# A selective scan that reads delta·u·B from PSUM, with B broadcast as three bfloat16 parts

## The chip, the cores and the metric

The kernel runs on one core of one Trainium2 chip. The metric is the device time of one execution in microseconds (us). Unless said otherwise, a time is the median of the runs of one kernel, and all runs used here are of the fast state. TensorE is called PE, its weight loads PEld, VectorE DVE, ScalarE ACT, GpSimd POOL. The granted clock is the share of TensorE's full clock that the profile records as granted; every entry of the record in the two traces before and after is 1 or 0.5, and a mean over a stretch lies between.

## The reference, cut to what matters

The block normalizes, projects and convolves its input, runs a selective scan in four directions (K = 4) over 4096 positions, and ends in linear attention and a quantized FFN. The argument touches only the scan:

```python
def step(h, inps):                       # for each position, N = 16 states n
    d_t, u_t, b_t, c_t = inps            # delta, u, B, C
    h = h * jnp.exp(d_t[..., None] * A) + (d_t * u_t)[..., None] * b_t[:, :, None, :]
    y = jnp.einsum('bkdn,bkn->bkd', h, c_t)
    return (h, y)
```

## The kernel before

Three passes: pass 1 makes u, B, C and the inputs of delta; pass 2 scans; pass 3 is the rest. Pass 2 works in 96 *steps*. A step is 128 (batch, channel) rows, one direction and T = 2048 positions. Each step has 16 *states* n, and halfway through it prepares the next step (delta, delta·u). A pair of batches gives three chunks of 128 rows; "third chunk" below is the one that holds rows of both batches.

```python
for n in range(N):
    if n == N // 2 and at + 1 < len(steps):
        ...
        ready = prepare(next_u, *steps[at + 1])       # delta, delta * u of the next step
    ct = more.tile([P, T], F32, name="ct")            # C's row n, broadcast by DMA
    ...
    da = two.tile([P, T], F32, name="da")
    nc.scalar.activation(da, delta, AF.Exp, scale=a_neg[:, ty, k, n : n + 1])
    dbu = two.tile([P, T], F32, name="dbu")                            # SBUF
    for hf in range(2):
        pb = ps.tile([P, HT], F32, name="pb", tag="wide")              # PSUM: B on all partitions
        for q in range(0, HT, GRP):
            nc.tensor.matmul(pb[:, q : q + GRP], spread(n, c), xd[...], start=True, stop=True)
        nc.vector.tensor_mul(dbu[:, sub], du[:, sub], pb)
    h = two.tile([P, T], F32, name="h")
    nc.vector.tensor_tensor_scan(h[:, way], da[:, way], dbu[:, way], init, ALU.mult, ALU.add)
    ...
    nc.gpsimd.tensor_mul(ct, ct, h)
    late.append(partial(sum_over_n, acc, ct, n, ...))  # PE adds ct into acc, LAG = 2 states late
```

`sum_over_n` is four fp32 matmuls of 512 columns by an identity matrix, which the profile counts as eight instructions (12,288 for the 1,536 states). "The sums" below are these.

Of the kernel before, what the change touches and what calls it, by code (L numbers as in the profile page):

```python
"""VSS block (group norm, gated depthwise conv, four-direction selective scan) followed by a linear
attention block and an e5m2/fp16-quantized FFN, on one core.

Three passes with DRAM scratch between them, in float32 throughout (e5m2 operands and float16
results where the reference quantizes to those formats):
  1. per pair of batches, channels on partitions: group norm, in_proj, conv + silu -> u; x_proj -> dt,
     B, C in each direction's scan order; silu(z) with tokens on partitions.
  2. per chunk of 128 (batch, channel) rows: the four scans, one state n at a time along the free
     axis. ScalarE makes exp(delta*A), TensorE broadcasts B over partitions and sums h*C over n in
     PSUM, VectorE scans, GpSimd multiplies by C. Reversed directions scan through reversed views.  # L10
  3. per batch, tokens on partitions: layer norm, gate, out_proj, residual; attention without
     softmax, reassociated: y = [ln,1] (Wq blockdiag(Wk^T [ln,1]^T[ln,1] Wv) Wff) + bff; quantized FFN.

A pair's 2*192 channel rows are three chunks of 128: (b0, 0:128), (b1, 0:128), and channels 128:192 of
both (b0 in the lower half). "Type" 0 / 1 below are parameters of channels 0:128 / 128:192 twice.
"""
# [9 lines left out]
F32 = mybir.dt.float32  # L26
F16 = mybir.dt.float16
F8 = mybir.dt.float8e5
AF = mybir.ActivationFunctionType
ALU = mybir.AluOpType  # L30
PSUM = bass.MemoryType.PSUM
DRAM = bass.MemoryType.DRAM

P = 128
NB, HH, WW, C = 8, 64, 64, 96
L = HH * WW
DI, N, R, K = 192, 16, 6, 4
NXD = R + 2 * N
NBLK = L // P
T = 2048  # L40
# [10 lines left out]
def chunk_rows(pair, c):  # L51
    """(partition slice, batch, channel slice) of a chunk's parts."""
    b0 = 2 * pair
    if c < 2:
        return [(slice(0, P), b0 + c, slice(0, P))]
    return [(slice(64 * j, 64 * j + 64), b0 + j, slice(P, DI)) for j in range(2)]


def load_by_type(nc, dst, src):
    """dst [128, 2, ...] from src [192, ...]: channels 0:128, and 128:192 twice."""  # L60
    nc.sync.dma_start(dst[:, 0], src[0:P])
    nc.sync.dma_start(dst[0:64, 1], src[P:DI])
    nc.sync.dma_start(dst[64:P, 1], src[P:DI])


@with_exitstack
def vss_attn_ffn_kernel(ctx: ExitStack, tc: tile.TileContext, g: dict, out: bass.AP):
    nc = tc.nc
    consts = ctx.enter_context(tc.tile_pool(name="consts", bufs=1))
    dram = ctx.enter_context(tc.tile_pool(name="scratch", bufs=1, space=DRAM))  # L70

    ident = consts.tile([P, P], F32, name="ident")
    make_identity(nc, ident)
    mhalf = consts.tile([P, NBLK], F32, name="mhalf")
    nc.vector.memset(mhalf, -0.5)

    u_d = [dram.tile([DI, L], F32, name=f"u_d{b}") for b in range(NB)]
    y_d = [dram.tile([DI, L], F32, name=f"y_d{b}") for b in range(NB)]
    z_d = [dram.tile([P, NBLK, DI], F32, name=f"z_d{b}") for b in range(NB)]
    xd_d = [[dram.tile([2 * NXD, L], F32, name=f"xd_d{b}_{o}") for o in range(2)] for b in range(NB)]  # L80

    def rsqrt_eps(var, eps):
        """var <- (var + eps) ** -0.5"""
        nc.gpsimd.tensor_scalar(var, var, eps, None, ALU.add)  # L84
        nc.gpsimd.tensor_tensor(var, var, mhalf[0 : var.shape[0], 0 : var.shape[1]], ALU.pow)  # L85

    pass1(tc, g, consts, ident, rsqrt_eps, u_d, z_d, xd_d)
    pass2(tc, g, ident, u_d, xd_d, y_d)
    pass3(tc, g, ident, rsqrt_eps, y_d, z_d, out)


@with_exitstack
def pass1(ctx, tc, g, consts, ident, rsqrt_eps, u_d, z_d, xd_d):
    nc = tc.nc
    wp = ctx.enter_context(tc.tile_pool(name="p1w", bufs=1))
    big = ctx.enter_context(tc.tile_pool(name="p1big", bufs=1))
    two = ctx.enter_context(tc.tile_pool(name="p1two", bufs=2))
    ps = ctx.enter_context(tc.tile_pool(name="p1ps", bufs=2, space=PSUM))

# [18 lines left out]
    for pair in range(NB // 2):  # L118
# [64 lines left out]
        for j in range(2):  # L183
            b = 2 * pair + j
            half = slice(64 * j, 64 * j + 64)
            for o in range(2):
# [13 lines left out]
                nc.sync.dma_start(xd_d[b][o], xd)  # L200


@with_exitstack
def pass2(ctx, tc, g, ident, u_d, xd_d, y_d):
    nc = tc.nc
    ND = R + N
    HT = T // 2
# [16 lines left out]
    load_by_type(nc, dt_b, g["dt_biasT"])  # L224
    # Rows as in the xd tile below: (dt, B) of batch 0, then of batch 1.
    dt_w = wp.tile([2 * ND, 3, K, P], F32, name="dt_w")
    nc.vector.memset(dt_w, 0.0)
    src = g["dt_wT"]
    nc.sync.dma_start(dt_w[0:R, 0], src[:, :, 0:P])
    nc.sync.dma_start(dt_w[ND : ND + R, 1], src[:, :, 0:P])  # L230
    nc.sync.dma_start(dt_w[0:R, 2, :, 0:64], src[:, :, P:DI])
    nc.sync.dma_start(dt_w[ND : ND + R, 2, :, 64:P], src[:, :, P:DI])

    spread2 = wp.tile([2 * ND, N, P], F32, name="spread2")
    for j in range(2):
        rows = ident[0 : 2 * ND, j * ND + R : (j + 1) * ND]
        nc.vector.tensor_copy(spread2[:, :, 64 * j : 64 * j + 64], rows.unsqueeze(2).to_broadcast([2 * ND, N, 64]))

    def spread(n, c):
        """Stationary operand that puts B's row n of a chunk's batches on all of their partitions."""  # L240
        if c < 2:
            row = c * ND + R + n
            return ident[0 : 2 * ND, row : row + 1].to_broadcast([2 * ND, P])
        return spread2[:, n, :]

    def piece(t, o, pc):
        """A piece of a [P, L] tile in row-major order, in the direction's order."""
        if o == 0:
# [10 lines left out]
    def prepare(u, pair, c, k, pc):  # L259
        """What a piece's states share: (dt, B) rows of its batches, delta, delta * u."""  # L260
        o, row0, cols = k % 2, (k // 2) * NXD, slice(pc * T, (pc + 1) * T)
        xd = two.tile([2 * ND, T], F32, name="xd")
        for j in range(2):
            nc.sync.dma_start(xd[j * ND : (j + 1) * ND, :], xd_d[2 * pair + j][o][row0 : row0 + ND, cols])
        # delta = softplus(v) = max(v, 0) + log1p(exp(-|v|)), the latter as
        # ln(w) + (e - (w - 1)) with w = 1 + e rounded.
        bias = dt_b[:, c // 2, k : k + 1]
# [17 lines left out]
        nc.gpsimd.tensor_mul(du.rearrange("p (a b) -> p a b", b=HH), delta.rearrange("p (a b) -> p a b", b=HH), piece(u, o, pc))  # L285
        return xd, delta, du

# [8 lines left out]
    ]  # L296
    # The sums over n are issued late, so that TensorE's broadcasts for the next states do not
    # stand behind them.
    late = []
    next_u = load_u(0, 0)  # L300
    ready = prepare(next_u, *steps[0])
    for at, (pair, c, k, pc) in enumerate(steps):
# [7 lines left out]
        if first:  # L310
            carry = two.tile([P, N], F32, name="carry")
        xd, delta, du = ready
        acc = ps_acc.tile([P, T], F32, name="acc")
        for n in range(N):
# [4 lines left out]
            ct = more.tile([P, T], F32, name="ct")  # L319
            row = (k // 2) * NXD + ND + n  # L320
            for part, b, _ in parts:
# [3 lines left out]
            nc.scalar.activation(da, delta, AF.Exp, scale=a_neg[:, ty, k, n : n + 1])  # L325
            dbu = two.tile([P, T], F32, name="dbu")
            for hf in range(2):
                pb = ps.tile([P, HT], F32, name="pb", tag="wide")
                for q in range(0, HT, GRP):
                    nc.tensor.matmul(pb[:, q : q + GRP], spread(n, c), xd[:, hf * HT + q : hf * HT + q + GRP], start=True, stop=True)  # L330
                sub = slice(hf * HT, (hf + 1) * HT)
                nc.vector.tensor_mul(dbu[:, sub], du[:, sub], pb)  # L332
            h = two.tile([P, T], F32, name="h")
            way = slice(None, None, -1) if rev else slice(None)
            init = 0.0 if first else carry[:, n : n + 1]
            nc.vector.tensor_tensor_scan(h[:, way], da[:, way], dbu[:, way], init, ALU.mult, ALU.add)  # L336
            if not final:
# [14 lines left out]
def pass3(ctx, tc, g, ident, rsqrt_eps, y_d, z_d, out):  # L352
# [43 lines left out]
    def normalize(dst, src, st, width, eps):  # L396
        """dst <- layer norm of src [P, blocks, width], from its bn_stats st [P, blocks, 6]."""
        nb = src.shape[1]
# [12 lines left out]
    for b in range(NB):  # L411
# [49 lines left out]

        # Attention without softmax.
        ln = two.tile([P, NBLK, CA], F32, name="ln")
# [37 lines left out]

        # FFN: e5m2 operands, float16 results.
        lf = two.tile([P, NBLK, CA], F32, name="lf", tag="ln")
# [71 lines left out]
```

## Time and profile before

| | us |
|---|---|
| whole kernel, median of 2 runs | 19,455.6 (19,454.37 to 19,456.82) |
| up to the first scan | 1,376 |
| pass 2, from the start of the first scan to the end of the last | 16,314 |
| one step of 16 states | 170 |
| a scan of 2048: alone / beside POOL | 4.48 / 6.57 |

Almost everything is pass 2. The busy times of that stretch, from the table of windows (columns: stretch, its length, busy time and number of instructions of PE, PEld, DVE, ACT and POOL, granted clock, DMA share, GB/s):

```profile
1376.00:17690.00 16314.00, 13637.42 (x25319) 5161.20 (x25318) 13842.94 (x4891) 4458.98 (x3453) 9915.15 (x2215) 0.82 0.34 104
```

PE and DVE are both busy about 84% of it, and neither figure can be taken at its word. A scan that stands still for POOL counts as busy (the prediction shows it): 6.57 us beside a POOL product, 4.48 alone. This standing still is called *the lock* below, a name for what was measured and for no mechanism. And PE's busy time depends on the clock it was granted: the matmul instructions of the sums start 0.429 us apart at full clock and 0.853 at half (medians, from 2,000 to 14,000 us).

### The profile page before, as it was taken

Reading aid. Unit: us, or ns where it says so; the run is one execution under the profiler, and the core shown is the slowest. Engines: PE = TensorE matmul, PEld = TensorE weight load, DVE = VectorE, ACT = ScalarE, POOL = GpSimd, SP = SyncE. Lnnn points to the kernel's source line nnn. Section 1 sums busy time; section 2 is a strip of 40 time slices with the busy share of each in tenths; the row PEclk is TensorE's granted clock in tenths of the full one; section 3 lists DMA queues with packets and bytes.
Section 4 is the critical chain, followed back from the end, with each engine's and each line's share of the span. In section 5 each row is a group of like instructions: output and inputs, shape, how many; then the busy total and the mean of one; then the engine's idle time right before and its main releaser. Section 6 shows DMA issues by size and latency. Waiting matters only on the chain. (4 is left out here: it accounts for less than half of the span.)

```text
span 19457.8 us, 87704 instructions
## 1 busy us (share of the span) xinstructions
PE 15569.7 (80%) x31520; PEld 6174.6 (32%) x31520; DVE 15130.4 (78%) x8039; ACT 5060.0 (26%) x4444; POOL 10511.8 (54%) x2562
## 2 busy tenths in 40 slices
PE   6668888888888888888888888888888888886555
PEld 2123333333333333333333333333333333333443
DVE  4448888888888888888888888888888888885344
ACT  2222222222222222222222222222222222221111
POOL 0016666655666665566666566666655666663323
PEclk5558888888888888888888888888888888886555
DMA  2112232244432322344322222444223223443110
GB/s 73 60 71 106 100 108 102 103 106 101 109 102 102 106 101 104 108 104 101 106 102 103 108 99 109 102 102 106 101 104 108 103 100 103 100 101 89 46 41 26
DMA packets 303310, 1860.89 MB, mean 96 GB/s; under 512 B 74891, under 2 KB 84060, under 8 KB 91100
## 3 DMA queue, kind: packets, MB, share of 16 engines
q1 hardware_dynamic: 292764, 1792.38, 30.4%
q0 software_dynamic: 10112, 62.92, 1.0%
q8 instruction: 249, 4.08, 0.1%
q14 instruction: 185, 1.52, 0.0%
HBM read 1747.14 MB, written 108.00 MB: 95 GB/s over the span
## 5 line engine op out<-in xcount | busy, mean ns | idle before, releaser
L340 POOL TENSOR_TENSOR ct<-ct,h 128x2048 f32<-128x2048 f32 x1536 | 7746.1, 5046 | 5654.8 <-DVE h L336 4720.5
L290 PE MATMUL acc<-ct,ident 128*128 128x512 f32 x12288 | 7138.9, 731 | 1598.4 <-POOL ct L340 1049.1
L336 DVE TENSOR_TENSOR_SCAN h<-da,dbu 128x2048 f32<-128x2048 f32 x768 | 4918.7, 6405 | 276.5 <-POOL ct L340 199.7
L336 DVE TENSOR_TENSOR_SCAN h<-da,carry,dbu 128x2048 f32<-128x2048 f32 x768 | 4891.8, 6370 | 268.7 <-POOL ct L340 188.7
L330 PE MATMUL pb<-xd,ident 44*128 44x512 f32 x8192 | 4219.8, 658 | 714.7 <-ACT delta L276 400.7
L332 DVE TENSOR_TENSOR dbu<-du,pb 128x1024 f32<-128x1024 f32 x3072 | 3605.2, 1203 | 1344.5 <-PE pb L330 1331.4
L290 PEld LDWEIGHTS acc<-ct,ident 128*128 128x128 f32 x12288 | 2699.4, 233 | 6060.2 <-issue 4451.8
L325 ACT ACTIVATE da<-delta,a_neg 128x2048 f32<-128x2048 f32 x1536 | 3073.6, 2001 | 5344.8 <-DVE h L336 5340.7
L330 PEld LDWEIGHTS pb<-xd,ident 44*128 44x128 f32 x8192 | 1554.5, 200 | 3258.3 <-issue 2100.7
L330 PE MATMUL pb<-xd,spread 44*128 44x512 f32 x4096 | 2100.8, 656 | 339.3 <-ACT delta L276 189.5
L339 ACT COPY carry<-h 128x1 f32<-128x1 f32 x768 | 147.1, 192 | 5373.6 <-DVE h L336 5373.6
L330 PEld LDWEIGHTS pb<-xd,spread 44*128 44x128 f32 x4096 | 774.6, 200 | 1604.3 <-issue 1044.3
L282 POOL TENSOR_TENSOR w<-w,e 128x1024 f32<-128x1024 f32 x192 | 735.0, 3828 | 577.7 <-ACT w L281 577.7
L279 POOL TENSOR_SCALAR w<-e 128x1024 f32<-128x1024 f32 x192 | 531.5, 2768 | 262.6 <-ACT e L277 262.6
L280 DVE SCALAR_TENSOR_TENSOR e<-w,e 128x1024 f32<-128x1024 f32 x192 | 234.6, 1222 | 512.5 <-POOL w L279 512.5
L285 POOL TENSOR_TENSOR du<-delta,u 128x2048 f32<-128x2048 f32 x96 | 481.1, 5011 | 0.1
L84 POOL TENSOR_SCALAR rstd<-rstd 128x16 f32<-128x16 f32 (+1 forms) x32 | 8.9, 277 | 853.1 <-DVE rstd L403 853.1
L283 POOL TENSOR_TENSOR delta<-delta,w 128x1024 f32<-128x1024 f32 x192 | 451.0, 2349 | 15.1
L273 PE MATMUL pd<-xd,dt_w 44*128 44x512 f32 x768 | 389.5, 650 | 77.4 <-DVE dbu L332 47.4
L281 ACT ACTIVATE w<-w 128x1024 f32<-128x1024 f32 x192 | 202.8, 1057 | 891.0 <-DVE e L280 891.0
L178 DVE SCALAR_TENSOR_TENSOR u<-xpad,conv_w,u 128x4096 f32<-128x4096 f32 x96 | 424.4, 4473 | 0.3
L292 DVE TENSOR_TENSOR y<-y,acc 128x2048 f32<-128x2048 f32 x96 | 327.8, 3415 | 122.0 <-PE acc L290 122.0
(134 smaller groups left out, 6608.4 us busy)
## 6 DMA issues: line engine op xcount, KB each, us to landing
ct<-xd_d SPq DMA_DIRECT2D x1024, 1024.0 KB
ct<-xd_d SPq DMA_DIRECT2D x1024, 512.0 KB
xd<-xd_d SPq DMA_DIRECT2D x192, 176.0 KB
z_d<-z POOLq DMA_DIRECT2D x64, 384.0 KB, 2.6
zs<-z_d SPq DMA_DIRECT2D x16, 1536.0 KB
xd_d<-xd SPq DMA_DIRECT2D x16, 1216.0 KB
u_d<-u SPq DMA_DIRECT2D x8, 2048.0 KB
u<-u_d SPq DMA_DIRECT2D x8, 2048.0 KB
```

What stands on the lines that cost most here:

```text
L178: nc.vector.scalar_tensor_tensor(uv, win, wt, uv, ALU.mult, ALU.add)
L273: nc.tensor.matmul(pd[:, q : q + GRP], dt_w[:, c, k, :], xd[:, hf * HT + q : hf * HT + q + GRP], start=True, stop=True)
L279: nc.gpsimd.tensor_scalar(w, e, 1.0, None, ALU.add)
L282: nc.gpsimd.tensor_sub(w, w, e)
L283: nc.gpsimd.tensor_add(delta[:, sub], delta[:, sub], w)
L285: nc.gpsimd.tensor_mul(du.rearrange("p (a b) -> p a b", b=HH), delta.rearrange("p (a b) -> p a b", b=HH), piece(u, o, pc))
L290: nc.tensor.matmul(acc[:, q : q + GRP], ident, ct[:, q : q + GRP], start=n == 0, stop=n == N - 1)
L325: nc.scalar.activation(da, delta, AF.Exp, scale=a_neg[:, ty, k, n : n + 1])
L330: nc.tensor.matmul(pb[:, q : q + GRP], spread(n, c), xd[:, hf * HT + q : hf * HT + q + GRP], start=True, stop=True)
L332: nc.vector.tensor_mul(dbu[:, sub], du[:, sub], pb)
L336: nc.vector.tensor_tensor_scan(h[:, way], da[:, way], dbu[:, way], init, ALU.mult, ALU.add)
L340: nc.gpsimd.tensor_mul(ct, ct, h)
```

## The change

Its intent: the scan takes delta·u·B straight from PSUM, where the product is made in place, so the scan has only one SBUF input; and B goes to PE as three bfloat16 parts that add up to the fp32 value exactly, so that one bf16 matmul takes the place of a pair of fp32 ones (12,288 broadcast instructions in the profile before, 6,144 in the one after).

```diff
+                part = b3.tile([2 * NXD, 3, L], BF16, name="part")                    # pass 1
+                nc.scalar.copy(part[:, 0, :], xd)
+                nc.gpsimd.tensor_sub(xd, xd, part[:, 0, :])
+                nc.scalar.copy(part[:, 1, :], xd)
+                nc.gpsimd.tensor_sub(part[:, 2, :], xd, part[:, 1, :])
+                nc.sync.dma_start(b3_d[b][o].rearrange("s r l -> r s l"), part)
...
-            dbu = two.tile([P, T], F32, name="dbu")
-            for hf in range(2):
-                pb = ps.tile([P, HT], F32, name="pb", tag="wide")
-                for q in range(0, HT, GRP):
-                    nc.tensor.matmul(pb[:, q : q + GRP], spread(n, c), xd[:, hf * HT + q : hf * HT + q + GRP], start=True, stop=True)
-                sub = slice(hf * HT, (hf + 1) * HT)
-                nc.vector.tensor_mul(dbu[:, sub], du[:, sub], pb)
...
+            halves = [slice(hf * HT, (hf + 1) * HT) for hf in ((1, 0) if rev else (0, 1))]
+            dbus = []
+            for sub in halves:
+                dbu = ps.tile([P, HT], F32, name="dbu", tag="wide")
+                for q in range(0, HT, GRP):
+                    nc.tensor.matmul(dbu[:, q : q + GRP], spread[:, c, n, :], b3[:, sub.start + q : sub.start + q + GRP], start=True, stop=True)
+                nc.vector.tensor_mul(dbu, du[:, sub], dbu)
+                dbus.append(dbu)
             init = 0.0 if first else carry[:, n : n + 1]
-            nc.vector.tensor_tensor_scan(h[:, way], da[:, way], dbu[:, way], init, ALU.mult, ALU.add)
+            for sub, dbu in zip(halves, dbus):
+                nc.vector.tensor_tensor_scan(h[:, sub][:, way], da[:, sub][:, way], dbu[:, way], init, ALU.mult, ALU.add)
+                end = sub.start if rev else sub.stop - 1
+                init = h[:, end : end + 1]
```

The PSUM buffers keep their sizes (acc with 2048 fp32 columns, and two of 1024 that held pb and now hold dbu), so the scan is cut into two halves of 1024, and each of the two is now held until its half scan has ended, not only until the product.

More of the change, by code (lines that the diff above doesn't have):

```diff
@@ L27 @@
 F16 = mybir.dt.float16
+BF16 = mybir.dt.bfloat16
 F8 = mybir.dt.float8e5
@@ L80, in vss_attn_ffn_kernel @@
     xd_d = [[dram.tile([2 * NXD, L], F32, name=f"xd_d{b}_{o}") for o in range(2)] for b in range(NB)]
+    b3_d = [[dram.tile([3, 2 * NXD, L], BF16, name=f"b3_d{b}_{o}") for o in range(2)] for b in range(NB)]
     def rsqrt_eps(var, eps):
@@ L85, in rsqrt_eps, with pass1 @@
         nc.gpsimd.tensor_tensor(var, var, mhalf[0 : var.shape[0], 0 : var.shape[1]], ALU.pow)
-    pass1(tc, g, consts, ident, rsqrt_eps, u_d, z_d, xd_d)
-    pass2(tc, g, ident, u_d, xd_d, y_d)
+    pass1(tc, g, consts, ident, rsqrt_eps, u_d, z_d, xd_d, b3_d)
+    pass2(tc, g, ident, u_d, xd_d, b3_d, y_d)
     pass3(tc, g, ident, rsqrt_eps, y_d, z_d, out)
 @with_exitstack
-def pass1(ctx, tc, g, consts, ident, rsqrt_eps, u_d, z_d, xd_d):
+def pass1(ctx, tc, g, consts, ident, rsqrt_eps, u_d, z_d, xd_d, b3_d):
     nc = tc.nc
@@ L97, in pass1 @@
     two = ctx.enter_context(tc.tile_pool(name="p1two", bufs=2))
+    b3 = ctx.enter_context(tc.tile_pool(name="p1b3", bufs=1))
     ps = ctx.enter_context(tc.tile_pool(name="p1ps", bufs=2, space=PSUM))
@@ L200, in pass1, with pass2 @@
                 nc.sync.dma_start(xd_d[b][o], xd)
+                part = b3.tile([2 * NXD, 3, L], BF16, name="part")
[4 more added lines that the diff above has]
+                nc.sync.dma_start(b3_d[b][o].rearrange("s r l -> r s l"), part)
 @with_exitstack
-def pass2(ctx, tc, g, ident, u_d, xd_d, y_d):
+def pass2(ctx, tc, g, ident, u_d, xd_d, b3_d, y_d):
     nc = tc.nc
-    ND = R + N
     HT = T // 2
@@ L224, in pass2 @@
     load_by_type(nc, dt_b, g["dt_biasT"])
-    dt_w = wp.tile([2 * ND, 3, K, P], F32, name="dt_w")
+    dt_w = wp.tile([2 * R, 3, K, P], F32, name="dt_w")
     nc.vector.memset(dt_w, 0.0)
@@ L229, in pass2 @@
     nc.sync.dma_start(dt_w[0:R, 0], src[:, :, 0:P])
-    nc.sync.dma_start(dt_w[ND : ND + R, 1], src[:, :, 0:P])
+    nc.sync.dma_start(dt_w[R : 2 * R, 1], src[:, :, 0:P])
     nc.sync.dma_start(dt_w[0:R, 2, :, 0:64], src[:, :, P:DI])
-    nc.sync.dma_start(dt_w[ND : ND + R, 2, :, 64:P], src[:, :, P:DI])
-    spread2 = wp.tile([2 * ND, N, P], F32, name="spread2")
+    nc.sync.dma_start(dt_w[R : 2 * R, 2, :, 64:P], src[:, :, P:DI])
+    NR = 2 * 3 * N
+    rowsum = wp.tile([NR, 2, N], BF16, name="rowsum")
     for j in range(2):
-        rows = ident[0 : 2 * ND, j * ND + R : (j + 1) * ND]
-        nc.vector.tensor_copy(spread2[:, :, 64 * j : 64 * j + 64], rows.unsqueeze(2).to_broadcast([2 * ND, N, 64]))
-    def spread(n, c):
-        if c < 2:
-            row = c * ND + R + n
-            return ident[0 : 2 * ND, row : row + 1].to_broadcast([2 * ND, P])
-        return spread2[:, n, :]
+        cols = [ident[0:NR, (3 * j + s) * N : (3 * j + s + 1) * N] for s in range(3)]
+        nc.vector.tensor_add(rowsum[:, j, :], cols[0], cols[1])
+        nc.vector.tensor_add(rowsum[:, j, :], rowsum[:, j, :], cols[2])
+    spread = wp.tile([NR, 3, N, P], BF16, name="spread")
+    for c in range(3):
+        for half in range(2):
+            j = c if c < 2 else half
+            nc.vector.tensor_copy(
+                spread[:, c, :, 64 * half : 64 * half + 64], rowsum[:, j, :].unsqueeze(2).to_broadcast([NR, N, 64])
+            )
     def piece(t, o, pc):
@@ L261, in prepare @@
         o, row0, cols = k % 2, (k // 2) * NXD, slice(pc * T, (pc + 1) * T)
-        xd = two.tile([2 * ND, T], F32, name="xd")
+        xd = two.tile([2 * R, T], F32, name="xd")
+        b3 = two.tile([NR, T], BF16, name="b3")
         for j in range(2):
-            nc.sync.dma_start(xd[j * ND : (j + 1) * ND, :], xd_d[2 * pair + j][o][row0 : row0 + ND, cols])
+            nc.sync.dma_start(xd[j * R : (j + 1) * R, :], xd_d[2 * pair + j][o][row0 : row0 + R, cols])
+            for s in range(3):
+                r = (3 * j + s) * N
+                nc.sync.dma_start(b3[r : r + N, :], b3_d[2 * pair + j][o][s, row0 + R : row0 + R + N, cols])
         bias = dt_b[:, c // 2, k : k + 1]
@@ L285, in prepare @@
         nc.gpsimd.tensor_mul(du.rearrange("p (a b) -> p a b", b=HH), delta.rearrange("p (a b) -> p a b", b=HH), piece(u, o, pc))
-        return xd, delta, du
+        return b3, delta, du
     def sum_over_n(acc, ct, n, yp):
@@ L311, in pass2 @@
             carry = two.tile([P, N], F32, name="carry")
-        xd, delta, du = ready
+        b3, delta, du = ready
         acc = ps_acc.tile([P, T], F32, name="acc")
@@ L319, in pass2 @@
             ct = more.tile([P, T], F32, name="ct")
-            row = (k // 2) * NXD + ND + n
+            row = (k // 2) * NXD + R + N + n
             for part, b, _ in parts:
```

## The prediction

> **What bounds the kernel now.** First the page's busy times, then its groups of instructions.
>
> ```profile
> PE 15569.7 (80%) x31520; PEld 6174.6 (32%) x31520; DVE 15130.4 (78%) x8039; ACT 5060.0 (26%) x4444; POOL 10511.8 (54%) x2562
> ...
> L340 POOL TENSOR_TENSOR ct<-ct,h 128x2048 f32<-128x2048 f32 x1536 | 7746.1, 5046 | 5654.8 <-DVE h L336 4720.5
> L290 PE MATMUL acc<-ct,ident 128*128 128x512 f32 x12288 | 7138.9, 731 | 1598.4 <-POOL ct L340 1049.1
> L336 DVE TENSOR_TENSOR_SCAN h<-da,dbu 128x2048 f32<-128x2048 f32 x768 | 4918.7, 6405 | 276.5 <-POOL ct L340 199.7
> ...
> L330 PE MATMUL pb<-xd,ident 44*128 44x512 f32 x8192 | 4219.8, 658 | 714.7 <-ACT delta L276 400.7
> L332 DVE TENSOR_TENSOR dbu<-du,pb 128x1024 f32<-128x1024 f32 x3072 | 3605.2, 1203 | 1344.5 <-PE pb L330 1331.4
> ```
>
> PE and DVE look equally full, and nothing says which one sets the time. Pass 2 is where it is: the first and last scan stand at 1376 and 17690 us, so it takes 16,314 of 19,456 us: 1536 states (96 steps of 16), 170 us a step. The chain that ended last covers only the tail of pass 3 and is no help. So I went to the timeline of DVE and of POOL at the end of one step.
>
> ```profile
> 9039.22 6.57 DVE L336 TENSOR_TENSOR_SCAN h<-da,carry,dbu 128x2048 f32<-128x2048 f32 x1
> 9045.72 2.25 DVE L292 TENSOR_TENSOR y<-y,acc 128x2048 f32<-128x2048 f32 x1
> 9047.89 2.34 DVE L332 TENSOR_TENSOR dbu<-du,pb 128x1024 f32<-128x1024 f32 x2
> 9050.36 4.48 DVE L336 TENSOR_TENSOR_SCAN h<-da,carry,dbu 128x2048 f32<-128x2048 f32 x1
> ...
> 9064.51 2.37 DVE L332 TENSOR_TENSOR dbu<-du,pb 128x1024 f32<-128x1024 f32 x2
> ```
>
> ```profile
> 9036.98 4.53 POOL L340 TENSOR_TENSOR ct<-ct,h 128x2048 f32<-128x2048 f32 x1 [4.42 <-DVE h L336]
> 9045.92 4.54 POOL L340 TENSOR_TENSOR ct<-ct,h 128x2048 f32<-128x2048 f32 x1 [4.42 <-DVE h L336]
> ```
>
> The same scan takes 6.57 us or 4.48 us. The 6.57 one began at 9039.22 while POOL multiplied until 9041.51; 9041.51 + 4.3 is its end. The 4.48 one began as POOL ended (9050.36 against 9050.46). So a "busy" scan first stands still until POOL is done. The muls and the y add, which read one operand from PSUM, lie fully beside POOL and keep their 1.16 us and 2.25 us. The steady period is 8.95 us: POOL's 4.53 plus the free scan's 4.40, start to start, one after the other; the two muls (2.32) hide beside POOL. Of the 1536 scans only 264 last under 4.6 us; the mean is 6.39, so some 2.0 us x 1536 = 3,050 us of DVE's "busy" time is standing still. The rest of a step, 170 - 16 x 8.95 = 27 us, lies around the preparation of the next step:
>
> ```profile
> DVE dbu L332 <- PE pb L330: 1331.4, 530, 8.0
> DVE e L280 <- POOL w L279: 478.6, 95, 5.2
> DVE h L336 <- POOL ct L340: 388.4, 190, 2.1
> DVE y L292 <- PE acc L290: 111.9, 11, 10.3
> ```
>
> (DVE's waits within pass 2: us, times, longest.) That is 24 us a step.
>
> [...] 4.40 us for 2048 elements is twice the 2.25 us of the y add. [...] I cut the clock record into its 3.41 us windows and weighted matmul time by active rows/128: below about 0.38 a fast window is followed by a slow one, and a slow one ends only after about 0.75. So matmuls of 44 rows hardly count, and passes 1 and 3 run at 0.56.
>
> **The change part by part.**
>
> *The lock goes (-2.1 us a state).* The scan now has da in SBUF and dbu in PSUM, like the mul that does not block. Then scan and POOL overlap.
>
> *The scan in two halves.* [...] a half costs about 2.27, with PSUM say 2.3 (estimate). The muls write PSUM instead of SBUF; I keep 1.16 to 1.2. DVE per state: 2 x 2.3 + 2 x 1.2 = 7.0 us. This becomes the bound; POOL needs 4.53 + 20/16 (prepare: 2 x (2.77 + 2.34 + 2.35) + 5.0 a step) = 5.8.
>
> *TensorE.* A pair of fp32 matmul instructions (each 0.427 us from start to start at full clock) becomes one bf16 one. [...]
>
> *The dbu buffers live longer.* There are still two, and each is now held from broadcast to end of scan. Does this close a loop through PE? I read the instruction order of the built kernel. Its usual DVE order is scan1(n-1), scan0(n), mul1(n), mul0(n+1), and on PE broadcast1(n), broadcast0(n+1), then the four sums. From the end of scan1(n-1) as 0: broadcast1(n) 0.1-0.5; scan0(n) until 2.3; broadcast0(n+1) 2.4-2.9, needed at 3.5; sums 2.9-6.4, next broadcast due at 7.0. It fits, and one slow-clock window (1.7 us of work lost) fits as well. In the third chunk of each pair the order is mul0, mul1, scan0, scan1 with both broadcasts ahead of the sums: that also closes at 7.1 to 7.2. So 16 states cost 112 us (third chunk 115).
>
> *Around the preparation* I walked one step by the order and the durations above. The y add costs 3.4 (its mean), the two corrections e 2.4. DVE's idle: 2.7 while pd sits in a dbu buffer until ScalarE's two reads of 1.1 are done; 3.5 until w (a POOL ct of 4.53, then 2.77) releases e; 0.7 for the next broadcast; 2.7 for the second e; 2.4 because du and two ct stand in front of the h buffer: 12 in all. In the third chunk pd waits behind all sums and the same walk gives some 8 more. With 3 to 5 for clock and latencies I have not drawn: 134 us for 64 steps, 145 for 32, mean 137.5, against 170. The saving in pass 2 is 32 x 96 = 3,100 us.
>
> *Pass 1* gains 16 groups of two ScalarE copies (about 3.7 us, from the 4096-wide activation) and two POOL subtractions (4 x 2.34 = 9.4). They lie beside an x_proj phase bound by PE (one 512-column pair per 3.83 us), but the parts have one buffer, so 26 us plus the store against 31 per group: about +60 us. The 768 extra loads of b3 are small. DMA's mean share was 0.60 in a steady stretch; at 7.0 us per state it becomes 0.77, still no bound.
>
> Sum: 1,311 + 60 (pass 1) + 75 (first preparation and set-up) + 96 x 137.5 = 13,200 + 15 + 1,753 (pass 3, unchanged) = 16,414. I put 16,450.
>
> **The rivals.**
>
> *PE's slow clock takes the place of the lock.* For: preparation matmuls of 12 rows count for almost nothing, and between broadcasts PE idles near 2 us, so windows under 0.38 will come. If half of all states ran at the PE-bound 8.8 us, a step would cost 0.5 x 16 x 1.8 = 14 more: 17,800. Against: a slow stretch fills PE, which passes 0.75 after one window.
>
> *PSUM in place is slower than I take it*, or the scan still locks. No DVE instruction of the trace reads and writes PSUM at once. At 2.2 us a mul the state costs 9.0 and the total is about 19,400; a scan that still locked would cost each state 4.53 + 4.6 = 9.1 or more, about 19,700. Against: the y add, with one SBUF and one PSUM input, ran beside POOL unhindered.
>
> *The waits of the preparation are hidden*, since DVE has no lock and POOL more slack: with only 5 us of idle a step instead of 12 to 20, 15,500.
>
> *The intent in the title, that broadcasts in bf16 are what pays*, would give little by itself: DVE waits for pb only 14 us a step, so at most 1,330 us, and the lock would still hold the 8.95.
>
> **Range and chances.** The error in a state (7.0 +- 0.25, 1536 times) is 380 us, that of a step's idle (+- 6, 96 times) 580, and unseen waits more often add: 15,700 to 17,350. Faster by over 2% has 0.95: only a scan that still locks, or PSUM writes at half rate, undo it.
>
> **What would show it.** Scans of 1024 at 2.3 us with no second cluster one POOL instruction higher; POOL's ct at 4.53 always, none at 8.6; a steady period near 7.0 with DVE over 95% busy there; broadcast matmuls near 0.21 us apart; a granted clock in pass 2 of 0.7 to 0.8; the waits of dbu and e around each preparation, 12 to 20 us a step; pass 1 ending some 60 us later. I am wrong if scans cluster near 4.5 us, if a mul takes over 1.5 us, or if dbu waits for PE in the steady stretch.

## The result, and the profile after

The changed kernel takes 17,229.4 us (median of 2 runs, 17,225.3 to 17,233.6). The ratio to before is 0.8856, 95% interval 0.883 to 0.8882. A ratio here is the mean time of one kernel's fast runs over that of the other's in the same rounds, so it is not quite the ratio of the medians quoted. It is faster by 11.4%, inside the predicted range of 15,700 to 17,350, but 779 us above the predicted 16,450.

The page's busy times and groups after (columns: line, engine, operation, tiles, shapes, count, busy time, mean ns of one, idle time before and what ended most of it):

```profile
PE 11367.0 (66%) x25376; PEld 4558.2 (26%) x25376; DVE 12439.4 (72%) x9583; ACT 5165.8 (30%) x4476; POOL 9695.8 (56%) x2594
...
L364 POOL TENSOR_TENSOR ct<-ct,h 128x2048 f32<-128x2048 f32 x1536 | 6951.1, 4526 | 4310.2 <-DVE h L358 3659.7
L310 PE MATMUL acc<-ct,ident 128*128 128x512 f32 x12288 | 7481.4, 752 | 2533.3 <-POOL ct L364 2206.0
L354 DVE TENSOR_TENSOR dbu<-du,dbu 128x1024 f32<-128x1024 f32 x3072 | 3657.4, 1219 | 2384.2 <-PE dbu L353 2363.5
...
L358 DVE TENSOR_TENSOR_SCAN h<-da,h,dbu 128x1024 f32<-128x1024 f32 x1536 | 3599.7, 2344 | 26.6
L353 PE MATMUL dbu<-b,spread 96*128 96x512 bf16 x6144 | 2022.1, 420 | 1920.6 <-DVE h L358 1801.5
```

Three things can be read here. POOL's product has fallen from a mean of 5.046 to 4.526 us, near the 4.53 that it took at the median before; there 193 of the 1,536 took 8.64 us on average, now the longest takes 4.57. The scan halves take 2.34 us; over all 3072 of them the mean is 2.323 and the longest is under 2.4, so nothing stands still any more. And DVE's wait for PE has grown: 2,363 us of idle time before the product, where before it was 1,331. The row of windows for pass 2 (here up to the start of the last scan):

```profile
1450.00:15429.00 13979.00, 9496.78 (x19172) 3522.24 (x19172) 11073.90 (x6427) 4454.48 (x3453) 8834.58 (x2214) 0.81 0.41 122
```

Pass 2 has fallen from 16,314 to 13,979 us (some 9 us of it because the first figure runs to the end of the last scan), and a step from 170 to 146. Yet DVE is busy only 79% of it and PE 68%. No engine is full, so something makes them wait for each other. The chain is in the timelines of one stretch of steady states. DVE:

```profile
9079.78 2.34 DVE L358 TENSOR_TENSOR_SCAN h<-da,h,dbu 128x1024 f32<-128x1024 f32 x1
9082.04 2.26 DVE L358 TENSOR_TENSOR_SCAN h<-da,dbu 128x1024 f32<-128x1024 f32 x1
9087.35 2.36 DVE L354 TENSOR_TENSOR dbu<-du,dbu 128x1024 f32<-128x1024 f32 x2 [3.05 <-PE dbu L353]
9089.62 2.34 DVE L358 TENSOR_TENSOR_SCAN h<-da,h,dbu 128x1024 f32<-128x1024 f32 x1
9091.88 2.26 DVE L358 TENSOR_TENSOR_SCAN h<-da,dbu 128x1024 f32<-128x1024 f32 x1
9094.05 2.33 DVE L354 TENSOR_TENSOR dbu<-du,dbu 128x1024 f32<-128x1024 f32 x2
```

PE in the same stretch:

```profile
9077.68 0.60 PE L353 MATMUL dbu<-b,spread 96*128 96x512 bf16 x2 [1.57 <-DVE h L358]
9080.25 6.62 PE L310 MATMUL acc<-ct,ident 128*128 128x512 f32 x8 [1.97 <-POOL ct L364]
9086.72 1.03 PE L353 MATMUL dbu<-b,spread 96*128 96x512 bf16 x4
9087.58 3.60 PE L310 MATMUL acc<-ct,ident 128*128 128x512 f32 x8
9092.01 0.60 PE L353 MATMUL dbu<-b,spread 96*128 96x512 bf16 x2 [0.84 <-DVE h L358]
```

And the POOL product that PE waits for:

```profile
9075.67 4.53 POOL L364 TENSOR_TENSOR ct<-ct,h 128x2048 f32<-128x2048 f32 x1 [5.36 <-DVE h L358]
```

Read the three together. PE issues its two broadcasts, then the sums of a state whose product POOL ends only at 9080.20: PE stands 1.97 us. Its clock is halved by then (cut into windows as below, the one from 9075.93 to 9079.35 holds 10% of weighted matmul time, and the next two are slow), so the sums take 6.62 us instead of 3.60. The next broadcasts stand behind them, and DVE, done with its scans at 9084.30, gets the first only at 9087.35: 3.05 us lost. The next state runs at 6.7 us, for PE is full and has its clock back. Then it begins anew. In this part of a step (before the preparation, in the first two chunks of a pair) every other state lasts some 9 to 10 us, the ones between 6.7.

The slow clock comes and goes in this trace as the prediction read it from the trace of before. Take the stretch from 2,000 to 14,000 us of this trace in clock windows of 3.41 us (apart from the first and the last, all 1,752 stretches of one clock in its record are multiples of 3.413 us), and count each matmul with its time from start to start (0.427 us in fp32, 0.215 in bf16, double in a slow window; the traces' fp32 medians are 0.429 and 0.853, and the bf16 broadcasts stand 0.215 apart where they are closest, 0.225 at the median and 0.402 in slow windows), weighted by active rows/128. Of the fast windows under 0.3, 590 of 590 were followed by a slow one; of those at 0.4 or more, none of 1,380. Of the slow windows at 0.8 or more, all 681 were the last slow one; of those under 0.6, none of 514. In the trace of before the upper limit is less clean: 12 of 1,768 fast windows at 0.4 or more were followed by a slow one, none at 0.5 or more. By the prediction's two limits, 469 of its 479 fast windows under 0.38 were followed by a slow one and 18 of the 1,779 above; of its slow windows 478 of 488 at 0.75 or more were the last slow one, and 9 of 769 under that. The weight matters: of its 1,759 fast windows with 0.8 or more of plain matmul time 182 were followed by a slow one; weighted by rows/128, none of the 1,387 at 0.5 or more. By this weight a matmul of 44 rows counts a third (44/128 = 0.34); the prediction's "hardly count" is too strong.

So my theory after the result was: the lock is gone as foreseen, and what is missing is this loop over PE, POOL and the slow clock, which the order of the sums sets up. The rivals were that the PSUM part alone brings less or more than I thought (that is, that bf16 matters, or does not), that the clock alone or the place of the sums alone is the cause, and that the wait for w around the preparation (494 us, or 5.1 a step) is on the path.

### The profile page after: what moved, and what is told of

The parts are those of the page before. It is cut to its first block, busy times and chain, and to the rows that moved or that the text cites. A ratio compares the mean times of both kernels' runs of the same rounds, so it can differ in the third digit from the quotient of the medians.

```text
span 17223.5 us, 81528 instructions
## 1 busy us (share of the span) xinstructions
PE 11367.0 (66%) x25376; PEld 4558.2 (26%) x25376; DVE 12439.4 (72%) x9583; ACT 5165.8 (30%) x4476; POOL 9695.8 (56%) x2594
## 5 line engine op out<-in xcount | busy, mean ns | idle before, releaser
L364 POOL TENSOR_TENSOR ct<-ct,h 128x2048 f32<-128x2048 f32 x1536 | 6951.1, 4526 | 4310.2 <-DVE h L358 3659.7
L310 PE MATMUL acc<-ct,ident 128*128 128x512 f32 x12288 | 7481.4, 752 | 2533.3 <-POOL ct L364 2206.0
L354 DVE TENSOR_TENSOR dbu<-du,dbu 128x1024 f32<-128x1024 f32 x3072 | 3657.4, 1219 | 2384.2 <-PE dbu L353 2363.5
L358 DVE TENSOR_TENSOR_SCAN h<-da,h,dbu 128x1024 f32<-128x1024 f32 x1536 | 3599.7, 2344 | 26.6
L353 PE MATMUL dbu<-b,spread 96*128 96x512 bf16 x6144 | 2022.1, 420 | 1920.6 <-DVE h L358 1801.5
L358 DVE TENSOR_TENSOR_SCAN h<-da,carry,dbu 128x1024 f32<-128x1024 f32 x768 | 1792.2, 2334 | 48.4 <-POOL ct L364 36.1
L358 DVE TENSOR_TENSOR_SCAN h<-da,dbu 128x1024 f32<-128x1024 f32 x768 | 1745.5, 2273 | 54.8 <-POOL ct L364 41.6
L353 PEld LDWEIGHTS <-spread 96*128 96x128 bf16 x6144 | 507.8, 104 | 4097.7 <-DVE h L358 2922.1
L302 POOL TENSOR_TENSOR w<-w,e 128x1024 f32<-128x1024 f32 x192 | 451.4, 2351 | 505.8 <-ACT w L301 505.8
L300 DVE SCALAR_TENSOR_TENSOR e<-w,e 128x1024 f32<-128x1024 f32 x192 | 251.7, 1311 | 494.0 <-POOL w L299 494.0
L293 PE MATMUL pd<-xd,dt_w 12*128 12x512 f32 x768 | 472.8, 751 | 147.4 <-DMA b<-b_d 88.6
```

The costliest lines, as they stand in the source:

```text
L293: nc.tensor.matmul(pd[:, q : q + GRP], dt_w[:, c, k, :], xd[:, hf * HT + q : hf * HT + q + GRP], start=True, stop=True)
L302: nc.gpsimd.tensor_sub(w, w, e)
L310: nc.tensor.matmul(acc[:, q : q + GRP], ident, ct[:, q : q + GRP], start=n == 0, stop=n == N - 1)
L353: nc.tensor.matmul(dbu[:, q : q + GRP], spread[:, c, n, :], b3[:, sub.start + q : sub.start + q + GRP], start=True, stop=True)
L354: nc.vector.tensor_mul(dbu, du[:, sub], dbu)
L358: nc.vector.tensor_tensor_scan(h[:, sub][:, way], da[:, sub][:, way], dbu[:, way], init, ALU.mult, ALU.add)
```

## The experiments

Eleven kernels, each timed in three rounds beside the kernel before on the same chip; the medians of before in these jobs lay between 19,441 and 19,460 us. All results were correct.

| run | what it is | us | ratio to before | clock, whole run |
|---|---|---|---|---|
| psum_f32 | before + scan from PSUM only | 17,799 | 0.9148 | 0.789 |
| sbuf_bf16 | changed, scan from SBUF again | 19,417 | 0.9981 | 0.749 |
| (changed) | both | 17,229 | 0.8856 | 0.761 |
| rows128 | changed, operands padded to 128 rows | 17,057 | 0.8768 | 0.789 |
| rows128_x2 | rows128, every broadcast twice | 17,010 | 0.8744 | 0.823 |
| rows128_x3 | rows128, every broadcast three times | 16,992 | 0.8738 | 0.857 |
| rows128_x2s | rows128, twice in steady states only | 16,743 | 0.8605 | 0.822 |
| ordered | changed, order of the sums fixed | 16,121 | 0.8282 | 0.791 |
| ordered_f32 | ordered with fp32 broadcast | 17,296 | 0.8888 | 0.840 |
| ordered_rows128 | ordered + padding | 16,011 | 0.8226 | 0.823 |
| ordered_wact | ordered + w on ACT | 15,751 | 0.8098 | 0.790 |
| ordered_rows_wact | ordered + both | 15,396 | 0.7916 | 0.836 |

### The two parts of the change alone

psum_f32 is the kernel before with only the in-place product and the two half scans; B stays one fp32 row.

```diff
-                nc.vector.tensor_mul(dbu[:, sub], du[:, sub], pb)
...
-            nc.vector.tensor_tensor_scan(h[:, way], da[:, way], dbu[:, way], init, ALU.mult, ALU.add)
...
+                nc.vector.tensor_mul(dbu, du[:, sub], dbu)
...
+                nc.vector.tensor_tensor_scan(h[:, sub][:, way], da[:, sub][:, way], dbu[:, way], init, ALU.mult, ALU.add)
```

> The kernel before with only the scan changed: product in PSUM, two half scans, broadcast still by two fp32 matmul instructions. My theory ([...] TensorE has no room without the cheap broadcast): scans drop to 2.3 us each as in the changed kernel, POOL's multiplication stays at 4.53 us, but TensorE needs 6.8 us a state at full clock and its broadcasts of 44 rows bring the slow clock, so the time stays near the kernel before: 18,500 to 20,500, middle 19,300. Rival (the lock is all that mattered, the bf16 broadcast pays nothing): 17,200 to 17,900.

17,799.3 us (17,781 to 17,809), 0.9148 [0.9134, 0.9161]. My number was missed and the rival's range hit: the PSUM part alone brings 1,660 of the 2,226 us, some 75%. Its scans take 2.33 us, its POOL products 4.53. DVE's waits in it (columns: us in all, times, longest):

```profile
DVE dbu L334 <- PE dbu L333: 1933.4, 1012, 4.7
DVE e L280 <- POOL w L279: 1064.7, 192, 23.2
```

PE's wait for POOL's product is only 246 us here, for the build emitted the sums in an order further behind. What holds it is PE itself: busy 13,782 of the 14,615 us from 1,376 to 15,991, and DVE waits for a broadcast 1,012 times, 1.9 us each.

sbuf_bf16 is the changed kernel with the product back in SBUF and one scan.

```diff
-                nc.vector.tensor_mul(dbu, du[:, sub], dbu)
+                nc.vector.tensor_mul(dbu[:, sub], du[:, sub], pb)          # bf16 broadcast kept
```

> The changed kernel with the product put back into SBUF and one scan of 2048; the bf16 broadcast in three parts stays (the rows of xd have one buffer instead of two, to make room). My theory (the lock sets the pace): the two clusters of scans at 4.5 and 6.6 us come back, the steady period is 8.95 us again, only some of the waits for the broadcast go: 18,700 to 19,400. Rival (a cheaper broadcast is what pays): under 18,200.

19,416.8 us, 0.9981 [0.9966, 0.9996]; 17 us outside my range, and its sense confirmed: by itself, the bf16 broadcast pays 0.2%. The groups show why (the first is half of the scans):

```profile
L356 DVE TENSOR_TENSOR_SCAN h<-da,carry,dbu 128x2048 f32<-128x2048 f32 x768 | 4803.5, 6256 | 369.1 <-POOL ct L360 359.2
...
L350 PE MATMUL pb<-b,spread 96*128 96x512 bf16 x6144 | 2038.8, 430 | 2408.5 <-DVE dbu L352 1907.5 <-ACT delta L296 451.7 <-DMA b<-b_d 42.6
```

These scans still take a mean of 6.26 us, near the 6.37 of the same scans before, and PE's saved time is idle time: 2,408 us before the broadcasts. An engine that was not the bound was made faster. The 39 us are a net figure: in the trace a step of the first two chunks is 4.1 us shorter than before (166.3 against 170.4), one of the third 5.3 us longer (175.1 against 169.8), because its two states of the preparation take 42.9 us instead of 35.2. This run also has one buffer for xd instead of two; whether that or the emitted order costs the third chunk its 5 us was not tested.

### The order of the sums

ordered is the changed kernel with the sums a state later (LAG = 3) and pinned in PE's order: one of a state's four sums after the second broadcast of a state, three after the first broadcast of the next.

```diff
+                with tc.issue_after(last.ins):            # last: the broadcast just issued
+                    if i == 0 and len(late) == LAG:
+                        sum_over_n(late.pop(0), T)         # the remaining three
+                    elif i == 1 and len(late) >= LAG - 1:
+                        sum_over_n(late[0], GRP)           # one
```

> The changed kernel with the sums over n issued in a fixed place: one of the four after the second broadcast of a state, the other three after the first broadcast of the next, and of a state whose product by C is two states old at least (one more buffer of C). My theory (the 33 us of idle in a step against the 12 to 20 I predicted come from sums that wait in TensorE's queue for POOL's product of the state just scanned, with the next broadcast behind them, and from the slow clock that these gaps bring): TensorE's waits of sums for POOL fall from 2206 us to under 600, the states of 9 to 11 us in the first half of a step fall to about 6.8, time 15,900 to 16,500. Rival (all of it comes from the preparation of the next step): within 1% of 17,229.

16,120.6 us (16,077 to 16,133), 0.8282 [0.8269, 0.8295]: as expected, and another 1,109 us off the changed kernel. PE's timeline in steady states is now

```profile
9078.27 0.60 PE L355 MATMUL dbu<-b,spread 96*128 96x512 bf16 x2 [1.32 <-DVE h L365]
9078.71 1.02 PE L311 MATMUL acc<-ct,ident 128*128 128x512 f32 x2
9080.44 0.61 PE L355 MATMUL dbu<-b,spread 96*128 96x512 bf16 x2 [0.71 <-DVE h L365]
9080.89 2.74 PE L311 MATMUL acc<-ct,ident 128*128 128x512 f32 x6
```

with a period of 6.67 us, DVE's own. In this stretch no sum waits for POOL, and PE's idle time is cut into two short pieces a state. The waits (us, times, longest):

```profile
DVE dbu L356 <- PE dbu L355: 849.2, 536, 6.0
DVE e L300 <- POOL w L299: 537.5, 165, 81.4
```

DVE's wait for PE fell from 2,363 to 849 us, and PE's for POOL's product from 2,206 to 387. In the first two chunks the first seven states of a step took 50.7 us instead of 59.1.

In the third chunk they became slower, 58.2 us instead of 51.9. There the fixed order leaves PE a gap behind DVE in each state (PE, then DVE):

```profile
7262.87 0.60 PE L355 MATMUL dbu<-b,spread 96*128 96x512 bf16 x2 [2.71 <-DVE h L365]
7263.32 4.44 PE L311 MATMUL acc<-ct,ident 128*128 128x512 f32 x6
7268.22 1.23 DVE L356 TENSOR_TENSOR dbu<-du,dbu 128x1024 f32<-128x1024 f32 x1 [1.90 <-PE dbu L355]
```

No sum waits for POOL here, but after the gap the clock is halved, the sums take 4.44 us instead of 2.74, and DVE waits for the broadcast behind them. A step of the third chunk still gains, 139.9 us against 146.0, all of it from the preparation on. So the order was put right for 64 of the 96 steps.

ordered_f32 has the same order with the fp32 broadcast.

```diff
-    nc.tensor.matmul(dbu[...], spread[:, c, n, :], b3[...], ...)     # bf16 parts
+    nc.tensor.matmul(dbu[...], spread(n, c), xd[...], ...)           # fp32, as before the change
```

> The order of 'ordered' with the fp32 broadcast of the kernel before (no bf16 parts). Theory: the two parts of the change need each other; with fp32 pairs PE has 8 x 0.427 + 4 x 2 x 0.427 = 6.8 us of work a state at full clock against DVE's 6.7, so the order cannot help it much and every slow-clock window is lost: 17,200 to 17,900, near psum_f32 (17,799), states of 7.0 to 7.6 us. So bf16 would be worth some 1,100 to 1,700 us once the sums no longer block. Rival: only the order of the sums matters and the broadcast's type does not: 16,100 to 16,350, as 'ordered'.

17,296.4 us, 0.8888 [0.8873, 0.8903], states of 7.6 us: the theory's range, not the rival's. PE is the bound here, as the row for pass 2 shows:

```profile
1376.00:15491.00 14115.00, 13267.67 (x25309) 4624.98 (x25310) 11701.35 (x6428) 4455.76 (x3453) 8841.62 (x2214) 0.90 0.40 120
```

PE is busy 94% of the stretch at a clock of 0.90. So what bf16 is worth depends on what stands beside it: 39 us while the lock holds (19,456 to 19,417), 570 once the lock is gone (17,799 to 17,229), 1,176 once the order is fixed too (17,296 to 16,121). Only the last pair has the same fixed order on both sides; the 570 also holds the different places of the sums in the two builds (half of them begin over 6 us after their product's end in psum_f32, and at once, 0.05 us after it, in the changed kernel).

### The clock, or the place of the sums?

ordered removes most of the wait for POOL and also some of the slow windows (1,078 of 3,515 are slow, in the changed kernel 1,370). These runs try to keep one and change the other. rows128 pads the operands of the broadcast and of delta with zero rows to 128, so that they count in full by the weight above; the numbers computed do not change.

```diff
-    spread = wp.tile([NR, 3, N, P], BF16, name="spread")                 # NR = 96
+    spread = wp.tile([P, 3, N, P], BF16, name="spread")                  # 128; dt_w likewise
...
+        b3s.append(wp.tile([P, T], BF16, name=f"b3{i}"))
+        nc.vector.memset(b3s[i], 0.0)                                    # two buffers, xd likewise
```

> The changed kernel with the operands of the broadcast (96 rows) and of the delta matmul (12 rows) padded with rows of zeros to 128; no work is added on TensorE (the scheduler moves a few sums, a side effect). If the clock follows matmul time weighted by active rows, more windows stay above the limit: granted clock in pass 2 from 0.80 to 0.85 or more and the time 16,700 to 17,050. If it follows plain busy time, or the slow clock does not matter, clock and time stay within 0.5%.

17,057.4 us, 0.8768 [0.8753, 0.8783]: 1.0% better, the clock up from 0.761 to 0.789. That is just outside what I expected (16,700 to 17,050 us, and 0.85 in pass 2, where it is 0.84 from 2,000 to 14,000 us), and outside the rival's 0.5% too. Of the 172 us, 30 came before pass 2 and 24 after it in the profiled runs, and a few sums had moved in the emitted order, so this is weak evidence. In steady states the loop was still whole:

```profile
9078.59 6.28 PE L318 MATMUL acc<-ct,ident 128*128 128x512 f32 x8 [1.88 <-POOL ct L372]
```

With only two pairs of broadcasts between the sums, the gap is short of work even when it counts in full. So the next two kernels give PE useless work in the gap.

```diff
                 for q in range(0, HT, GRP):
+                    for _ in range(2):                     # 3 in rows128_x3
                         nc.tensor.matmul(dbu[...], spread[:, c, n, :], b3[...], start=True, stop=True)
```

> 'rows128' with each broadcast matmul issued twice, the second over the first: useless work on PE (some 0.9 us a state at full clock: 4.3 to 5.2 of DVE's 6.7), placed where PE otherwise idles before the sums. Theory A, that the slow clock is what lets the sums run past the next broadcast's due time: more work keeps windows above 0.38, sums take 3.6 instead of 6.3 us more often, and the kernel becomes faster with more work: 16,500 to 16,900 against 17,057, clock up from 0.789. Theory B, that the sums' standing behind GpSimd's product is enough by itself: no faster, 17,050 to 17,400.

> The same with each broadcast matmul three times (6.1 us of PE work a state). Theory A: nearly all windows of pass 2 stay fast, clock 0.87 or more, 16,300 to 16,800. Theory B: the extra work only makes the next broadcast later, 17,200 to 17,800, although the clock is up.

17,010.3 us (0.8744 [0.873, 0.8759]) and 16,992.4 us (0.8738 [0.8725, 0.8751]): neither theory's range was hit. A expected a gain of over 150 us, B none and a loss with 1.7 us more work a state. The traces show two opposite effects. In steady states of rows128_x2, PE runs so:

```profile
9054.60 3.70 PE L318 MATMUL acc<-ct,ident 128*128 128x512 f32 x8 [1.55 <-POOL ct L373]
9058.14 1.89 PE L362 MATMUL dbu<-b,spread 128*128 128x512 bf16 x8
9061.39 3.70 PE L318 MATMUL acc<-ct,ident 128*128 128x512 f32 x8 [1.36 <-POOL ct L373]
```

The sums still wait 1.4 to 1.55 us for POOL, and now in every state, but they take 3.70 us, and states last 6.8 to 7.2 us. That is A's picture: the wait alone fits into the period, and only with the slow clock does it not. But around the preparation (states 7 and 8) these kernels lost as much: 30.5 us in the first two chunks against 24.9 in rows128, 38.1 against 28.3 in the third. The build had emitted another order of PE's instructions there. So the totals could not decide. rows128_x2s repeats the broadcasts only for n < 6 or n > 10, which keeps the order around the preparation close to that of rows128.

```diff
-                    for _ in range(2):
+                    for _ in range(2 if n < 6 or n > 10 else 1):
```

> 'rows128_x2' came out at 17,010, its clock in pass 2 up from 0.84 to 0.88. By states it is not B: where it is steady the sums still wait 1.4 to 1.5 us for GpSimd's product, yet take 3.70 us, and states last 6.8 to 7.1 us; in chunks 0 and 1 of a pair the first seven states of a step fell from 58.7 to 53.3 us. But the two states in which the next step is prepared rose from 24.9 to 30.5 (third chunk 28.3 to 38.1), and there the compiler's order of PE had changed. This run repeats the broadcasts only in the states n < 6 and n > 10; the order around the preparation is then close to that of rows128. Theory A (slow clock decides in the steady states, the order around the preparation gave the gain back): first seven states 53 to 55 us, the two of the preparation under 27, total 16,400 to 16,750. Theory B (the sum's place behind the product decides): 16,950 to 17,200.

16,743.5 us (16,735 to 16,748), 0.8605 [0.8591, 0.8619]: inside A's range. The first seven states fell from 58.7 to 51.4 us, the two of the preparation stayed at 24.0 in the first two chunks (in the third 29.6, above my 27). PE's wait for POOL's product is still 1,936 us (rows128: 2,223). More useless work on PE made the kernel 314 us *faster*. That speaks for the clock: the wait for POOL makes the gap, and the halved clock after it is what makes the sums overrun. It is not perfectly clean, since the build also split some sums differently in steady states; rows128_x2's stretch above, where it did not, says the same. So do the states of ordered's third chunk, where the clock is lost and the broadcasts come late without any wait for POOL.

### The waits around the preparation

ordered_wact makes w = 1 + e on ACT instead of POOL; ordered_rows128 adds the padding to ordered; ordered_rows_wact does both.

```diff
-            nc.gpsimd.tensor_scalar(w, e, 1.0, None, ALU.add)
+            nc.scalar.activation(w, e, AF.Identity, bias=1.0)
```

> 'ordered' with w = 1 + e made by ScalarE instead of GpSimd. DVE's wait for w was 537.5 us there (5.6 a step, 96 steps): w stands in GpSimd's queue behind a ct product of 4.53 us. Theory: that wait is on the path, since DVE sets the pace in 'ordered'; it falls below 200 us and most of it is gained: 15,650 to 15,900 against 16,120. Rival: the wait only hides another (dbu for PE, or the h buffer for ct) that then ends last: 16,050 to 16,200, with those waits grown by what e's lost.

15,750.7 us, 0.8098 [0.8086, 0.811]: as expected. DVE's wait for w is 89 us (537 in ordered). Of the waits that remain, the first has grown by 102 us and the second has shrunk by 45 (849 and 399 us in ordered):

```profile
DVE dbu L356 <- PE dbu L355: 950.9, 580, 6.0
DVE h L365 <- POOL ct L371: 354.2, 95, 16.0
```

The gain is 370 us; in the profiled runs pass 2 is 328 us shorter and pass 3, where nothing was changed, 60. Set against 448 us less of waiting, most of the wait for w was on the path.

> 'ordered' with the operands of broadcast and delta padded to 128 rows (numbers unchanged). It gained 1.0% on the changed kernel, where slow windows were many (clock 0.761 to 0.789). Theory: in 'ordered' DVE sets the pace and slow windows are few in steady states, so only those around the preparation are left to gain: 15,950 to 16,100, clock from 0.791 to 0.82 or more. Rival: clock is still what a third of the steps loses; 15,700 to 15,900.

16,010.9 us, 0.8226 [0.8214, 0.8238], clock 0.823: 110 us, inside my range, of which some 40 came before the first scan (1,410 against 1,450 us). So padding is worth little here. That the slow clock costs little does not follow: the first seven states of the third chunk still take 56.2 us, against 50.3 to 50.9 in the others. The rival's time was not hit, but its picture, that a third of the steps loses by the clock, is nearer the trace than mine.

> Both of the last two on 'ordered'. Theory: the gains add: 15,500 to 15,800, the fastest of all. Rival: both remove the same idle time around the preparation: no faster than the better of the two alone.

15,395.7 us (15,362 to 15,431), 0.7916 [0.7899, 0.7933]: 104 us under my range; the gains add and more (370 + 110 = 480 us from the two alone, 725 found). It is the fastest version found: 20.8% below before and, by the two ratios (0.7916 / 0.8856), 10.6% below the changed kernel. Its pass 2:

```profile
1400.00:13585.00 12185.00, 8250.08 (x18822) 3169.11 (x19174) 11024.27 (x6428) 4634.60 (x3643) 8400.58 (x2024) 0.90 0.46 140
```

DVE is busy 90% of it. Now one engine is nearly full. Why the two add up to more than their sum was not tested.

## Why the prediction was right or wrong

It was right on direction and its main mechanism, and its range held the result. That it did is partly luck: the range allowed for "unseen waits", but not for the loop that came, and the result lies 121 us under its upper end. Point by point:

- **The lock goes**: right. All 3072 half scans lie between 2.2 and 2.4 us with no second cluster, and POOL's longest product is 4.57 us. psum_f32 (scans of 2.33 us) shows that this alone is 1,660 us; sbuf_bf16 shows the lock unchanged where the operand stays in SBUF (scans of 2048 at 6.26 us, 6.37 before).
- **The scan in two halves, the product in place**: right. 2.323 us (predicted 2.3) and 1.219 us (1.16 to 1.2; 1.203 before, with the result in SBUF). That a half would cost 2.27 us, more than half of the free scan's 4.40, the trace of before did not show. It came out: half scans start 2.26 us apart, so that two take 2 x 2.26 - 4.40 = 0.12 us more than the free scan. A state bound by DVE lasts 6.7 us, a little under the predicted 7.0, because start to start is shorter than the printed durations (2.26 against 2.32 for a half scan, 1.12 against 1.22 for a product).
- **Pass 1**: right. The first scan stands at 1,450 us; the prediction's sum was 1,311 + 60 + 75 = 1,446. From the start of the last scan on it took 19 us longer than before (1,795 against 1,776), where pass 3 was taken as unchanged. (The 17,690 us at which the prediction has the last scan of before is its end.)
- **Does this close a loop through PE?** This is the step that failed. The prediction put the sums at "2.9-6.4" after the end of the second half scan and concluded "It fits, and one slow-clock window (1.7 us of work lost) fits as well." It read PE's order right (broadcasts, then the sums), but took the sums' operand as ready. The sums are of the state whose scan has just ended. In the stretch shown the second half scan ends at 9075.44. From there, POOL's product of it ends at 4.8, so the sums begin at 4.8, not 2.9. At full clock they would end at about 8.4, and rows128_x2 shows that this still nearly fits (its states last 6.8 to 7.2 us, and DVE waits at most 0.46 us between 9,050 and 9,100 us). At half clock they end at 11.4, which does not. And the gap before them, a few broadcasts and then 1.97 us of nothing, is where the window lies after which the clock is halved (10% of weighted matmul time, then two slow windows); of the windows counted above 1,370 of 3,516 were slow. The error was not to ask when the sums' operand is ready: the slow clock was checked only for sums that begin at 2.9, and the wait for POOL not at all.
- **What that term measured**: the prediction had 134 us a step for the first two chunks and 145 for the third. Measured are 145.7, 146.3 and 146.0. So the third chunk, whose order the prediction walked separately, came out as predicted, and the 64 other steps took 12.0 us too long: 64 × 12.0 = 768 of the 779 us that pass 2 lies above the predicted 13,200. ordered, which removes the loop from the first two chunks, has 131.9 and 131.4 us there: below the predicted 134.
- **The waits around the preparation**: about right once the loop is taken out. DVE waits 24.6 us a step for PE (2,363.5 / 96) and 5.1 for w (494 / 96), together 30, where 12 to 20 were predicted; the excess is the loop. ordered has 8.8 and 5.6, together 14. So these waits are not hidden, as one rival had it.
- **The rivals**: "PE's slow clock takes the place of the lock" came true for every other state before the preparation in the first two chunks, and near its own size (14 us a step; 12 found). What was written against it, that "a slow stretch fills PE, which passes 0.75 after one window", held too: that is why only every other state is slow. One of the signs named as proof of error, "if dbu waits for PE in the steady stretch", appeared. That "broadcasts in bf16 are what pays" was rightly called small by itself (39 us), but the prediction did not see that its worth grows to 1,176 us once the lock is gone and the order fixed.
- **The signs**: broadcasts 0.215 us apart where they are closest (two more of them lengthen a group from 0.60 to 1.03 us) and a clock of 0.81 in pass 2 were as predicted to within 0.01. The trace of before had no such bf16 matmul to show this spacing. By the measured ones PE's work for a state is 8 x 0.429 + 4 x 0.215 = 4.3 us at full clock and 8 x 0.853 + 4 x 0.402 = 8.4 at half, against DVE's 6.7. DVE was busy 79% of pass 2, and in the stretch shown 82% (13.47 of the 16.52 us from 9079.78 to 9096.30), far from the 95% predicted.

## What to carry to other kernels

When a product moves into a buffer that is held longer, follow each instruction queue in its emitted order and ask of every instruction in front of the next producer not only how long it takes but when its own operand is ready; a short wait there can cost the clock as well (here a wait of 1.97 us, after which the sums took 6.62 us instead of 3.60). What a part of a change is worth is not a number of its own: the same bf16 broadcast was worth 39, 570 or 1,176 us, depending on what else held the kernel. An order that repairs the loop in one part of a kernel can open a gap in another, so look at each part. And where useless work made the kernel faster, and a fix of the order alone brought 6%, the bound was neither engine but the way they wait for each other.
